# Layer 0's LSTM weights: their sums made once and kept in DRAM, and a few small operations of a step put in another order

## The chip, the cores and the metric

The kernel runs on one core of a Trainium2 chip. TensorE (PE) multiplies matrices, VectorE (DVE), ScalarE (ACT) and GpSimd (POOL) do the elementwise work, SyncE (SP) starts most transfers between DRAM and the on-chip memory SBUF. Every engine works through its own list of instructions in a fixed order; an instruction that waits holds up all that stand behind it on that engine. The metric is the device time of one execution in microseconds (us), as a median over runs. All data is float32.

## The reference, cut to what matters

Four graph layers, each `x = x + layer(relu(layernorm(x)))`. The change touches layer 0 alone: two graph convolutions, and then an LSTM over windows of p = 1, 2, 3 and 4 time steps in turn, whose last state overwrites the window's last step.

```
h = relu(einsum('ts,bsh->bth', adj, x @ Wg0 + bg0))
h = relu(einsum('ts,bsh->bth', adj, h @ Wg1 + bg1))
for p in range(1, 5):
    wins = h[:, :nw * p, :].reshape(Bv * nw, p, Hd)
    last = _lstm_last(Wih[p - 1], Whh[p - 1], bih[p - 1], bhh[p - 1], wins)
    h = h.at[:, idx, :].set(last)

# one step of the LSTM
g = x_t @ Wih.T + h @ Whh.T + bias
i, f, gg, o = split(g, 4)
c = sigmoid(f) * c + sigmoid(i) * tanh(gg)
h = sigmoid(o) * tanh(c)
```

x has 8192 rows of 256. Wih and Whh have, for each p, 1024 x 256 numbers: 1024 KB in SBUF, 8 KB in each of the 128 partitions.

## The kernel before, in words

**The order of the program.** The instructions of an engine run in the order in which they are written, but one that isn't pinned may be placed ahead of others that were written before it. `late(ins)` (line 78) pins an instruction behind the one that was written just before it for the same engine; it says nothing of those written after it, which may still move up.

**Convolutions (lines 525 to 656).** The 8192 rows go through in 16 chunks of 512 (`NCH`). A loop over rounds n = 0 to 19 starts chunk n in round n; each chunk is a generator of five pieces (norm, aggregation, first product, second product, second aggregation), so that five chunks are under way at a time. Beside each piece, from round 3 on, one piece of `tables` is written: first `edge_tables` (line 297), which prepares layer 1, then `late_tables` (line 215), which prepares layers 2 and 3. The fourth piece of `late_tables` takes a power -0.5 on POOL (line 247, tile `dinv`), and its fifth copies `dinv` on DVE (line 250, `dinv_b`). Neither is pinned. By the count of pieces, 4 in round 3 and 5 in each of rounds 4 to 13, the fourth piece of `late_tables`, which is the 55th in all, is written in the first turn of round 14.

**The weights of the LSTM (lines 494 to 516).** Each matrix product is made from seven products of quarters instead of eight. For this the four quarters a11, a12, a21, a22 of a set of weights are joined by three sums and one difference, each a 128 x 512 operation on POOL (line 512). `Weights(kind, w)` loads a set (line 500, on SP's queue) and makes them. That happens 14 times: there are two halves of the data, each with phases w = 1, 2, 3, 4, so eight sets of `ih`, and six of `hh` (w = 1 needs none). Three are loaded in the second round of the convolutions (line 652), the rest during the LSTM: `hh` when a phase ends (`phase_over`, line 945) into a single buffer, `ih` eight slots later (line 1008) into one of two.

**The LSTM (lines 660 to 1031).** PE works through slots. A slot is a gate of a step: `product` (line 745) issues its seven products in several pieces, with the accumulators `pa`, `pb`, `pc` in PSUM read between the pieces by ACT (lines 795, 800) and DVE (796, 803, 806, 813); a product that adds to `pa` again must wait until `pa` was read (line 806). `prepare` (line 700) makes a step's seven right-hand sides from its inputs: copies (line 724), differences (lines 727, 737) and one more (742). Where the step before opens a phase, POOL makes them, else ACT and DVE. At the end of a step `gate_done` makes h and its differences on DVE (lines 865 to 869).

**Memory.** The chunk buffers of the convolutions and the LSTM's tiles use the same bytes one after the other; an LSTM tile waits only for the earlier users of its own bytes. The convolutions' region holds, in this order, `xin` (4 x 4096 bytes of a partition), `g0` (10 x 4096), `wc` (5408) and `hop` (3 x 4096). The LSTM lays over it `xop` and `hop2` (2 x 9408 each), `cp` (2 x 5376) and `gp`, eight gate tiles of 5376 bytes. In the memory map the gate tiles are handed out in the order first, eighth, seventh and so on down to the second.

Of the kernel before, what the change touches and what calls it, by code (L numbers as in the profile page):

```python
# [17 lines left out]
P = 128  # L18
# [13 lines left out]
def gnn_stack_kernel(ctx: ExitStack, tc: tile.TileContext, a: dict, out: bass.AP):  # L32
# [45 lines left out]
    def late(ins):  # L78

        tc.keep_in_program_order(ins)  # L80
# [404 lines left out]
    with ExitStack() as l0:  # L485
# [5 lines left out]

        class Weights:
            def __init__(self, kind, w, keep=lambda ins: None):
                bufs = 2 if kind == "ih" else 1
                t = wsp.tile([P, 2, 4, 2, P], F32, tag=f"w{kind}", name=f"w{kind}", bufs=bufs)
                s = wsp.tile([P, 3, 4, P], F32, tag=f"s{kind}", name=f"s{kind}", bufs=bufs)
                keep(
                    nc.sync.dma_start(  # L500
                        out=t.rearrange("p k q j m -> p k (q j m)"), in_=a[f"W{kind}T"][:, w - 1]
                    )
                )
                a11, a12, a21, a22 = t[:, 0, :, 0, :], t[:, 1, :, 0, :], t[:, 0, :, 1, :], t[:, 1, :, 1, :]
                s1, s2, s4 = s[:, 0], s[:, 1], s[:, 2]
                for o, x, y, op in (
                    (s1, a21, a22, ALU.add),
                    (s2, s1, a11, ALU.subtract),
                    (s4, a12, s2, ALU.subtract),
                    (a21, a11, a21, ALU.subtract),  # L510
                ):
                    keep(nc.gpsimd.tensor_tensor(o, x, y, op))  # L512
                self.of = {1: a11, 2: a12, 3: s4, 4: a22, 5: s1, 6: s2, 7: a21}

            def __call__(self, k, q):
                return self.of[k][:, q, :]

        bias = w0.tile([P, MAX_SKIP, 8], F32, tag="bias", name="bias")
        bias2 = w0.tile([P, MAX_SKIP, 8], F32, tag="bias2", name="bias2")
# [5 lines left out]
        with ExitStack() as conv:  # L525
# [111 lines left out]

            tables = chain(edge_tables(), late_tables())
            under_way = []
            for n in range(NCH + 4):  # L640
                if n < NCH:
                    under_way.append(graph_convolutions(n))

                turns = under_way[-1:] + under_way[:-1] if n < NCH else list(under_way)
                if n == 1:
                    turns += under_way[-1:]
                for one in turns:
                    if next(one, 0) == 0:
                        under_way.remove(one)
                    if n >= 3:  # L650
                        next(tables, None)
                if n == 2:
                    weights["ih", 0], weights["ih", 1] = Weights("ih", 1), Weights("ih", 2)
                    weights["hh", 1] = Weights("hh", 2)
                    late(nc.vector.tensor_tensor(bias, bias, bias2, ALU.add))
            for _ in tables:
                pass


# [17 lines left out]
        class Step:  # L677
# [22 lines left out]
            def prepare(self, beside):  # L700
# [22 lines left out]
                def copied(to, k):  # L723
                    copy(self.as_nodes(v[:, to : to + 1]), self.nodes(slice(k, k + 1), t))  # L724

                def difference(to, k, l):
# [5 lines left out]
                    )  # L732

                copied(0, 0)
                difference(3, 2, 0)
                copied(1, 1)
                sums(
                    self.as_nodes(v[:, 5:6]), self.nodes(slice(3, 4), t), self.as_nodes(v[:, 3:4]), ALU.subtract
                )
                copied(2, 3)  # L740
                difference(4, 3, 2)
                sums(v[:, 6], v[:, 1], v[:, 5], ALU.subtract)
                self.x = {1: v[:, 0], 2: v[:, 1], 3: v[:, 2], 4: v[:, 6], 5: v[:, 3], 6: v[:, 5], 7: v[:, 4]}

# [82 lines left out]
            def gate_done(self, q):  # L827
# [28 lines left out]
                elif last:  # L856
                    if self.halved:
                        return
                    o_, g_ = (act[k][0].rearrange("p (q n) -> p q n", n=N) for k in (3, 2))
                    nc.vector.tensor_tensor(  # L860
                        self.nodes(slice(0, 4), t), self.as_nodes(o_), self.as_nodes(g_), ALU.mult
                    )
                else:
                    h = hop.tile([P, 7 * NMAX], F32, tag="h", name="lstm_h")
                    nc.vector.tensor_tensor(h[:, : 4 * N], act[3][0], act[2][0], ALU.mult)
                    v = h[:, : 7 * N].rearrange("p (q n) -> p q n", n=N)
                    nc.vector.tensor_tensor(v[:, 4:6], v[:, 2:4], v[:, 0:3:2], ALU.subtract)
                    nc.vector.tensor_tensor(v[:, 6], v[:, 3], v[:, 4], ALU.subtract)
                    nc.vector.tensor_tensor(v[:, 2], v[:, 1], v[:, 6], ALU.subtract)
                    state["h"] = {1: v[:, 0], 2: v[:, 1], 3: v[:, 3], 4: v[:, 2], 5: v[:, 4], 6: v[:, 6], 7: v[:, 5]}  # L870

# [87 lines left out]
        for slot in range(len(tasks) + 2):  # L959
# [45 lines left out]
            next(norm_steps, None)  # L1005
            while later_weights and later_weights[0][0] <= slot:
                _, ph = later_weights.pop(0)
                weights["ih", ph] = Weights("ih", phases[ph], late)
            if old:
                (at, q, k), step = old[0], steps[old[0][0]]  # L1010
                if k == len(step.gates) - 1:
                    if at + 1 == len(steps) or steps[at + 1].phase != step.phase:
                        phase_over(step.phase)
                    if step.phase == len(phases) - 1 and step.t == 1 and step.g == NGR - 1:

                        t_ = wsp.tile([P, 2, 4, 2, P], F32, tag="wih", name="x_first", bufs=2)
                        flat = t_.rearrange("p k q j m -> p k (q j m)")
                        norms1 = {}
                        for n in range(2):
                            xt = flat[:, n, :].rearrange("p (i d) -> p i d", i=4)  # L1020
# [1315 lines left out]
```

## Time and profile before

| what | us |
|---|---|
| median of 3 runs | 1943.82 (1942.74 to 1943.88) |
| the profiled execution, its own time | 1939.26 |
| span of its profile, first to last instruction | 1937.5 |
| convolutions, on PE | 0 to 190 |
| LSTM, on PE | 190 to 1253 |
| weights' sums on POOL (line 512), 56 operations | 17.9 to 33.1 and 281 to 1096 |
| one sum, 128 x 512, alone | 1.27 |
| one load of a set of weights, issue to landing | `ih` 7.0, `hh` 5.3 (medians) |

The span is what the profile shows of one execution; its own time is 1.8 us longer, which lies around it. Busy times are sums over the span; in lists of waits the three numbers are the time in all, the number of waits and the longest. In a timeline each line has start, duration, engine, line of the code and what was done, and in square brackets the idle time of the engine before it with what ended that. "SPq" and "POOLq" are the parts of SP and POOL that start transfers.

### The profile page before, as it was taken

Reading aid. Unit: us, or ns where it says so; the run is one execution under the profiler, and the core shown is the slowest. Engines: PE = TensorE matmul, PEld = TensorE weight load, DVE = VectorE, ACT = ScalarE, POOL = GpSimd, SP = SyncE. Lnnn points to the kernel's source line nnn. Section 1 sums busy time; section 2 is a strip of 40 time slices with the busy share of each in tenths; the row PEclk is TensorE's granted clock in tenths of the full one; section 3 lists DMA queues with packets and bytes.
Section 4 is the critical chain, followed back from the end, with each engine's and each line's share of the span. In section 5 each row is a group of like instructions: output and inputs, shape, how many; then the busy total and the mean of one; then the engine's idle time right before and its main releaser. Section 6 shows DMA issues by size and latency. Waiting matters only on the chain. (4 is left out here: it accounts for less than half of the span.)

```text
span 1937.5 us, 25232 instructions
## 1 busy us (share of the span) xinstructions
PE 1910.5 (99%) x9146; PEld 1394.8 (72%) x9146; DVE 1328.0 (69%) x2529; ACT 1165.4 (60%) x2199; POOL 465.5 (24%) x616
## 2 busy tenths in 40 slices
PE   9999999999999999999999999999999999999998
PEld 7777468866678884688666788876676875544787
DVE  8774675674575557756745655688788877787886
ACT  4353775664565547756645656488887556592554
POOL 3000031140040003311400200056776420000584
PEclk9999999999999999999999999999999999999999
DMA  8513000010010035000100100342323841022112
GB/s 264 186 50 109 0 23 1 1 44 0 1 44 1 1 127 178 22 1 1 44 1 1 44 1 11 99 163 104 136 61 118 329 164 57 1 72 81 43 66 88
DMA packets 63276, 132.56 MB, mean 68 GB/s; under 512 B 6576, under 2 KB 41520, under 8 KB 60848
## 3 DMA queue, kind: packets, MB, share of 16 engines
q1 hardware_dynamic: 59072, 119.22, 18.0%
q0 software_dynamic: 3472, 11.54, 1.6%
q8 instruction: 72, 1.18, 0.3%
q14 instruction: 52, 0.43, 0.1%
q10 hardware_dynamic: 608, 0.20, 0.1%
HBM read 86.10 MB, written 44.83 MB: 68 GB/s over the span
## 5 line engine op out<-in xcount | busy, mean ns | idle before, releaser
L780 ACT ACTIVATE gate<-gate,bias 128x256 f32<-128x256 f32 (+2 forms) x368 | 247.7, 678 | 174.4 <-DVE gate L796 89.5
L752 PE MATMUL pa<-xop,sih 128*128 128x256 f32 (+2 forms) x1056 | 342.3, 417 | 4.8 <-DVE gate L806 4.6
L752 PEld LDWEIGHTS pa<-xop,sih 128*128 128x128 f32 x1056 | 198.7, 190 | 74.9 <-issue 19.1
L752 PE MATMUL pc<-xop,wih 128*128 128x256 f32 (+2 forms) x736 | 251.2, 423 | 0.0
L796 DVE TENSOR_TENSOR gate<-pb,gate 128x256 f32<-128x256 f32 (+2 forms) x184 | 87.6, 476 | 226.5 <-PE pb L752 147.6
L752 PE MATMUL pa<-lstm_h,shh 128*128 128x256 f32 (+1 forms) x672 | 212.7, 398 | 0.0
L752 PEld LDWEIGHTS pc<-xop,wih 128*128 128x128 f32 x736 | 139.8, 190 | 51.2 <-issue 22.5
L813 DVE TENSOR_TENSOR gate<-pc,gate 128x256 f32<-128x256 f32 (+2 forms) x184 | 87.6, 476 | 115.1 <-PE pc L752 114.0
L752 PEld LDWEIGHTS pa<-lstm_h,shh 128*128 128x128 f32 x672 | 127.7, 190 | 30.1
L1162 ACT ACTIVATE lr<-pair 128x1024 f32<-128x1024 f32 x128 | 124.2, 1023 | 40.1 <-ACT xv L1146 16.8
L752 PE MATMUL pc<-lstm_h,whh 128*128 128x256 f32 (+1 forms) x448 | 141.8, 398 | 0.0
L795 ACT COPY gate<-pa 128x256 f32<-128x256 f32 (+2 forms) x184 | 76.0, 413 | 86.8 <-PE pa L752 86.7
L1127 PE MATMUL bank<-wlv,hT 128*128 128x260 f32 x480 | 115.6, 382 | 1.7 <-DVE xq L1138 1.7
L806 DVE TENSOR_TENSOR gate<-pa,gate 128x256 f32<-128x256 f32 (+2 forms) x184 | 87.5, 476 | 40.9 <-PE pa L752 40.1
L780 ACT ACTIVATE gate<-pa,bias 128x256 f32<-128x256 f32 (+2 forms) x184 | 93.8, 510 | 28.9 <-PE pa L752 26.9
L800 ACT COPY gate<-pa 128x256 f32<-128x256 f32 (+2 forms) x184 | 75.2, 409 | 55.7 <-PE pa L752 54.7
L752 PE MATMUL pb<-xop,wih 128*128 128x256 f32 (+1 forms) x320 | 101.8, 400 | 1.6 <-POOL xop L724 1.2
L752 PE MATMUL pa<-xop,wih 128*128 128x256 f32 (+1 forms) x320 | 101.3, 398 | 0.1
L1127 PEld LDWEIGHTS bank<-wlv,hT 128*128 128x128 f32 x480 | 88.2, 190 | 16.6 <-DVE xq L1138 3.6
L752 PEld LDWEIGHTS pc<-lstm_h,whh 128*128 128x128 f32 x448 | 85.1, 190 | 20.1
L512 POOL TENSOR_TENSOR shh<-whh 128x512 f32<-128x512 f32 x6 | 7.7, 1276 | 379.1 <-DMA whh<-in_WhhT 193.2
L724 POOL COPY xop<-hT 128x256 f32<-128x256 f32 (+1 forms) x36 | 30.8, 856 | 275.6 <-ACT gate L780 261.4
(395 smaller groups left out, 4051.1 us busy)
## 6 DMA issues: line engine op xcount, KB each, us to landing
field<-keep SPq DMA_DIRECT2D x4, 2304.0 KB, 12.3
wih<-in_WihT SPq DMA_DIRECT2D x8, 1024.0 KB, 7.0
xres<-in_x SPq DMA_DIRECT2D x16, 512.0 KB, 4.5
xa<-xres POOLq DMA_DIRECT2D x16, 512.0 KB, 4.8
xin<-xb SPq DMA_DIRECT2D x16, 512.0 KB, 3.7
h<-xb SPq DMA_DIRECT2D x16, 512.0 KB, 3.6
xin<-in_x SPq DMA_DIRECT2D x15, 512.0 KB, 5.6
out_x<-h SPq DMA_DIRECT2D x15, 512.0 KB, 2.9
```

What stands on the lines that cost most here:

```text
L512: keep(nc.gpsimd.tensor_tensor(o, x, y, op))
L724: copy(self.as_nodes(v[:, to : to + 1]), self.nodes(slice(k, k + 1), t))
L752: ins = nc.tensor.matmul(p[:, : self.N], weights[kind, self.phase](k, q), x[k], start=first_ and kind == "ih", stop=kind == "hh" or not se ...
L780: nc.scalar.activation(out, in_, AF.Tanh if q == 2 else AF.Sigmoid, bias=bias[:, self.w - 1, 2 * q + j : 2 * q + j + 1],)
L795: nc.scalar.copy(blk[0, 0], pa[:, :N])
L796: nc.vector.tensor_tensor(blk[0, 0], pb[:, :N], blk[0, 0], ALU.add)
L800: nc.scalar.copy(blk[1, 0], pa[:, :N])
L806: nc.vector.tensor_tensor(blk[1, 1], pa[:, :N], blk[1, 1], ALU.add)
L813: nc.vector.tensor_tensor(blk[1, 0], pc[:, :N], blk[1, 0], ALU.add)
L1127: ins = nc.tensor.matmul(o, hTs[n][:, k, i * P : (i + 1) * P], wlv[:, k, cols], start=k == 0, stop=k == 1)
L1162: nc.scalar.activation(lr, p, AF.Relu)
```

## The change

It has three parts. One: a set of weights and its sums now lie in one tile of 14 KB a partition. The three sets that are needed first are loaded behind round 7, each in two parts, summed once and, behind round 8, also written to DRAM (`keep_sums`). The sets of w = 3 and 4 are loaded in eight parts, from round 9 on and one part in five turns, into one buffer (`ahead`), summed on POOL and written to DRAM; loads and stores of these go through POOL's queue. In the LSTM a set comes from DRAM with its sums, in one transfer. Two: in `prepare` the second copy is made before the first difference, and the third difference before the third copy. Three: the difference of two blocks of h becomes two differences of one block, the second of them behind the next one.

```diff
@@ -491,29 +491,57 @@
 
 
+        PART = 14 * P
+        quarters0 = {
+            (kind, w): dram.tile([P, 2, PART], F32, tag=f"q{kind}{w}", name=f"q{kind}{w}")
+            for kind in ("ih", "hh")
+            for w in range(1, MAX_SKIP + 1)
+        }
+
+        def load_part(v, kind, w, part, queue):
+            at = slice(part * 4 * P, (part + 1) * 4 * P)
+            return queue.dma_start(
+                out=v[:, : 8 * P].rearrange("p (k x) -> p k x", k=2), in_=a[f"W{kind}T"][:, w - 1, :, at]
+            )
+
+        def quarters(v):
+            t = v[..., : 8 * P].rearrange("p h (k q j m) -> p h k q j m", k=2, q=2, j=2)
+            s1, s2, s4 = (
+                v[..., (8 + 2 * k) * P : (10 + 2 * k) * P].rearrange("p h (q m) -> p h q m", q=2) for k in range(3)
+            )
+            a11, a12, a21, a22 = (t[:, :, k, :, j, :] for j, k in ((0, 0), (0, 1), (1, 0), (1, 1)))
+            return a11, a12, s4, a22, s1, s2, a21
+
+        def sum_quarters(v, keep=lambda ins: None):
+            a11, a12, s4, a22, s1, s2, a21 = quarters(v)
+            for o, x, y, op in (
+                (s1, a21, a22, ALU.add),
+                (s2, s1, a11, ALU.subtract),
+                (s4, a12, s2, ALU.subtract),
+                (a21, a11, a21, ALU.subtract),
+            ):
+                keep(nc.gpsimd.tensor_tensor(o, x, y, op))
+
         class Weights:
-            def __init__(self, kind, w, keep=lambda ins: None):
-                bufs = 2 if kind == "ih" else 1
-                t = wsp.tile([P, 2, 4, 2, P], F32, tag=f"w{kind}", name=f"w{kind}", bufs=bufs)
-                s = wsp.tile([P, 3, 4, P], F32, tag=f"s{kind}", name=f"s{kind}", bufs=bufs)
-                keep(
-                    nc.sync.dma_start(
-                        out=t.rearrange("p k q j m -> p k (q j m)"), in_=a[f"W{kind}T"][:, w - 1]
-                    )
+            def __init__(self, kind, w, first_time=False, keep=lambda ins: None):
+                v = wsp.tile(
+                    [P, 2, PART], F32, tag=f"w{kind}", name=f"w{kind}", bufs=2 if kind == "ih" else 1
                 )
-                a11, a12, a21, a22 = t[:, 0, :, 0, :], t[:, 1, :, 0, :], t[:, 0, :, 1, :], t[:, 1, :, 1, :]
-                s1, s2, s4 = s[:, 0], s[:, 1], s[:, 2]
-                for o, x, y, op in (
-                    (s1, a21, a22, ALU.add),
-                    (s2, s1, a11, ALU.subtract),
-                    (s4, a12, s2, ALU.subtract),
-                    (a21, a11, a21, ALU.subtract),
-                ):
-                    keep(nc.gpsimd.tensor_tensor(o, x, y, op))
-                self.of = {1: a11, 2: a12, 3: s4, 4: a22, 5: s1, 6: s2, 7: a21}
+                self.of = quarters(v)
+                self.given = v, kind, w
+                if first_time:
+                    for part in range(2):
+                        keep(load_part(v[:, part], kind, w, part, nc.sync))
+                    sum_quarters(v, keep)
+                else:
+                    keep(nc.sync.dma_start(out=v, in_=quarters0[kind, w]))
+
+            def keep_sums(self):
+                v, kind, w = self.given
+                late(nc.gpsimd.dma_start(out=quarters0[kind, w], in_=v))
 
             def __call__(self, k, q):
-                return self.of[k][:, q, :]
+                return self.of[k - 1][:, q // 2, q % 2, :]
 
         bias = w0.tile([P, MAX_SKIP, 8], F32, tag="bias", name="bias")
         bias2 = w0.tile([P, MAX_SKIP, 8], F32, tag="bias2", name="bias2")
@@ -637,6 +665,19 @@
 
             tables = chain(edge_tables(), late_tables())
             under_way = []
+
+            def other_weights():
+                for kind, w, part in [(kind, w, part) for w in (3, 4) for kind in ("ih", "hh") for part in range(2)]:
+                    v = wc.tile([P, 1, PART], F32, tag="ahead", name="ahead")
+                    late(load_part(v[:, 0], kind, w, part, nc.gpsimd))
+                    for _ in range(3):
+                        yield
+                    sum_quarters(v, late)
+                    late(nc.gpsimd.dma_start(out=quarters0[kind, w][:, part : part + 1], in_=v))
+                    for _ in range(2):
+                        yield
+
+            ahead = other_weights()
             for n in range(NCH + 4):
                 if n < NCH:
                     under_way.append(graph_convolutions(n))
@@ -649,11 +690,17 @@
                         under_way.remove(one)
                     if n >= 3:
                         next(tables, None)
+                    if n >= 9:
+                        next(ahead, None)
+                if n == 8:
+                    for kept in weights.values():
+                        kept.keep_sums()
+                if n == 7:
+                    for kind, ph, w in (("ih", 0, 1), ("ih", 1, 2), ("hh", 1, 2)):
+                        weights[kind, ph] = Weights(kind, w, True, late)
                 if n == 2:
-                    weights["ih", 0], weights["ih", 1] = Weights("ih", 1), Weights("ih", 2)
-                    weights["hh", 1] = Weights("hh", 2)
                     late(nc.vector.tensor_tensor(bias, bias, bias2, ALU.add))
-            for _ in tables:
+            for _ in chain(tables, ahead):
                 pass
 
 
@@ -732,13 +779,13 @@
                     )
 
                 copied(0, 0)
+                copied(1, 1)
                 difference(3, 2, 0)
-                copied(1, 1)
                 sums(
                     self.as_nodes(v[:, 5:6]), self.nodes(slice(3, 4), t), self.as_nodes(v[:, 3:4]), ALU.subtract
                 )
+                difference(4, 3, 2)
                 copied(2, 3)
-                difference(4, 3, 2)
                 sums(v[:, 6], v[:, 1], v[:, 5], ALU.subtract)
                 self.x = {1: v[:, 0], 2: v[:, 1], 3: v[:, 2], 4: v[:, 6], 5: v[:, 3], 6: v[:, 5], 7: v[:, 4]}
 
@@ -864,8 +911,9 @@
                     h = hop.tile([P, 7 * NMAX], F32, tag="h", name="lstm_h")
                     nc.vector.tensor_tensor(h[:, : 4 * N], act[3][0], act[2][0], ALU.mult)
                     v = h[:, : 7 * N].rearrange("p (q n) -> p q n", n=N)
-                    nc.vector.tensor_tensor(v[:, 4:6], v[:, 2:4], v[:, 0:3:2], ALU.subtract)
+                    nc.vector.tensor_tensor(v[:, 4], v[:, 2], v[:, 0], ALU.subtract)
                     nc.vector.tensor_tensor(v[:, 6], v[:, 3], v[:, 4], ALU.subtract)
+                    nc.vector.tensor_tensor(v[:, 5], v[:, 3], v[:, 2], ALU.subtract)
                     nc.vector.tensor_tensor(v[:, 2], v[:, 1], v[:, 6], ALU.subtract)
                     state["h"] = {1: v[:, 0], 2: v[:, 1], 3: v[:, 3], 4: v[:, 2], 5: v[:, 4], 6: v[:, 6], 7: v[:, 5]}
 
@@ -1005,7 +1053,7 @@
             next(norm_steps, None)
             while later_weights and later_weights[0][0] <= slot:
                 _, ph = later_weights.pop(0)
-                weights["ih", ph] = Weights("ih", phases[ph], late)
+                weights["ih", ph] = Weights("ih", phases[ph], keep=late)
             if old:
                 (at, q, k), step = old[0], steps[old[0][0]]
                 if k == len(step.gates) - 1:
@@ -1013,8 +1061,8 @@
                         phase_over(step.phase)
                     if step.phase == len(phases) - 1 and step.t == 1 and step.g == NGR - 1:
 
-                        t_ = wsp.tile([P, 2, 4, 2, P], F32, tag="wih", name="x_first", bufs=2)
-                        flat = t_.rearrange("p k q j m -> p k (q j m)")
+                        t_ = wsp.tile([P, 2, PART], F32, tag="wih", name="x_first", bufs=2)
+                        flat = t_.rearrange("p h x -> p (h x)")[:, : 8 * D].rearrange("p (n x) -> p n x", n=2)
                         norms1 = {}
                         for n in range(2):
                             xt = flat[:, n, :].rearrange("p (i d) -> p i d", i=4)
```

## The prediction

> **What bounds the kernel.** I read the page first: busy shares and PE's clock.
>
> ```profile
> PE 1910.5 (99%) x9146; PEld 1394.8 (72%) x9146; DVE 1328.0 (69%) x2529; ACT 1165.4 (60%) x2199; POOL 465.5 (24%) x616
> ...
> PEclk9999999999999999999999999999999999999999
> ```
>
> PE works in all but 27 us (1937.5 - 1910.5), at full clock. The change leaves PE's matmuls alone, so it can save only out of these 27 us, and it costs whatever new idle time it gives to PE. POOL, which the change relieves, is busy a quarter of the time; its share as such is worth nothing. So the list of PE's waits came second. Its columns are time in all, number, longest.
>
> ```profile
> PE pa L752 <- DVE gate L806: 4.6, 8, 1.0
> ...
> PE pb L752 <- POOL xop L724: 1.2, 2, 0.6
> ```
>
> These are the LSTM's two large ones. No row has PE waiting for weights: the loads and sums were always in time. Third, the timeline around each wait. This is one at the end of phase w = 2:
>
> ```profile
> 406.24 1.27 POOL L512 TENSOR_TENSOR shh<-whh 128x512 f32<-128x512 f32 x1 [58.17 <-DMA whh<-in_WhhT]
> ...
> 406.46 1.41 DVE L742 TENSOR_TENSOR xop<-xop 128x336 f32<-128x336 f32 x1
> ...
> 408.21 0.49 DVE L806 TENSOR_TENSOR gate<-pa,gate 128x336 f32<-128x336 f32 x1
> ...
> 408.76 0.83 PE L752 MATMUL pa<-xop,sih 128*128 128x336 f32 x2 [0.80 <-DVE gate L806]
> ```
>
> Line 742 took 1.41 us where it takes 0.43 in the median; it ends at 407.87, 0.36 after the sum on POOL (406.24 + 1.27), not 0.43 after its own start. So a sum on POOL holds up a DVE operation with two inputs from SBUF, line 806 behind it is late, and PE waits. That is what the removed sums cost.
>
> **What it saves.** (a) 44 of the 56 sums (11 sets of 4) leave the LSTM. Waits of PE that stand behind such a held line 742: 0.80 at 408.76, 0.99 at 559.12, 0.93 at 941.17, together 2.7 us; at 559 the hold is 0.76 (1.19 - 0.43), so I take 2.5. The bounds are 0 (DVE finds another delay) and 2.9 (with 0.16 at 557.43).
> (b) The earlier second copy: two waits of 0.6, at 268.12 and 800.40, both for the copy that stands behind the first difference on POOL. It saves 1.2 at most. But the difference then meets the DVE operation of line 850 that starts at 266.35 (1.23 us), and the sixth product, which needs it, may wait 1.1 instead of 0.6: a loss of 1.0 for both. I take a gain of 0.5.
> (c) Line 867 in two: a block takes about 0.42 (line 868's form) against 0.67 for both, so DVE works 0.17 us longer a step, but what is needed first comes sooner and less is held at once (1.36 us at 279.04). The waits of 0.33, 0.33 and 0.32 at 281.67, 813.95 and 1101.29 may shrink: 0 to 1.0, I take 0.5.
> (d) In the convolutions, 12 sums leave the stretch 17.9 to 33.1. There DVE's line 106 took 1.22, 0.79 and 0.52 instead of 0.16. PE idles 1.9 us between 10 and 40 us (10 - 9.16 and 10 - 8.96, by windows of 10 us), partly for other reasons: 0 to 1.9, I take 0.8.
> Sum: 2.5 + 0.5 + 0.5 + 0.8 = 4.3 us.
>
> **What is hidden.** A load of 1.83 MB instead of 1.05 is 0.79 MB more, 1.9 us at the 426 GB/s of 405 to 407. The tightest use: `hh` is issued at 551.81, first used at 567.86. Together with the `ih` behind it, 3.67 MB take 8.6 us and some 2 us to start: 562.5, 5 us early. Without that cover each of the tight ones would cost what it is late. On SP's queue six loads of about 0.4 us move behind chunk 10's load; they delay chunk 11 by the 8 us of their bytes, from 72.6 to 81, and DVE reads it only at about 110.
>
> **What it adds: a chain on POOL in the convolutions.** Two lines of SP's timeline fix its start.
>
> ```profile
> 54.95 1.35 SPq L389 DMA_DIRECT2D field<-keep  x1
> 56.62 8.36 SPq L540 DMA_DIRECT2D xin<-in_x  x2
> ```
>
> The first sets are pinned behind chunk 10's load, issued at 56.62, which lands 14.6 us later, at 71.2, since the queue is full of `field` stores. Three sets, 3.15 MB, then take 8.1 us at the 387 GB/s of 64 to 66: the first is there at 73.9, the last at 79.3. POOL sums from 73.9 on: 12 x 1.27 = 15.3, to 89.2. Three stores are issued at 0.54 each (line 916), to 90.8; they move 5.5 MB, 14.2 us, to 105. The first part of the staging is loaded behind them on the same queue. Bounds: 94.7, if they don't hold it up (3.9 for 512 KB, line 540 at 71 to 115), and 107.8; I take 107.
> One part of the staging: load 3.9; four sums of 128 x 256 at 0.73 (line 737 on POOL) 2.9; store of 917 KB, which is 2.8 (`hm`, 512 KB) to 4.8 (`xa`, on POOL's queue) and 1.0 for the rest, say 4.6. There is one buffer, so nothing overlaps: 11.4 us a part, 10.6 to 12.6. The sums of parts three, four and five end at 132.7, 144.1 and 155.5, the last store lands at 194.3 (by the ends 176 to 205).
>
> **Who stands behind the waiting POOL.** (e) The root of the degrees, and DVE behind it:
>
> ```profile
> 134.25 0.58 POOL L247 TENSOR_TENSOR dinv<-dinv,half_power 128x1 f32<-128x1 f32 x1 [101.19 <-DMA a<-in_a]
> ```
> ```profile
> 135.94 0.21 DVE L250 COPY dinv_b<-dinv 128x128 f32<-128x128 f32 x1
> ...
> 136.79 0.69 DVE L618 TENSOR_TENSOR aggT<-bank,bg 128x512 f32<-128x512 f32 x1
> ```
>
> Line 247 is written in round 14, behind part five (25 turns from round 9) and ahead of part six, whose load is pinned behind it. It isn't pinned itself and may move up, but whatever part it ends up behind, POOL reaches it when that part is through. Behind part three or earlier it isn't late; behind four it is 10 us late, behind five 21. DVE then stops at line 250, and line 618, less than 1 us behind, empties a bank that PE needs. The eight PSUM banks give PE some 1 us. I take part four: a wait of 9 us, bounds 0 and 20.
> (f) Beside these, 44 sums on POOL now meet DVE between 74 and 195. In 90 to 110 DVE is busy 9.9 of 10 us, so a held operation (1.06 us for line 106 above) is passed on; elsewhere it is half idle. 0 to 5, I take 1.
> (g) The LSTM's gate tiles lie on the bytes of `ahead`. In the convolutions' region it takes 62,752 to 69,920 behind `xin`, `g0` and the rest of `wc`; the gate tiles start at 48,384, so the third and fourth and 32 bytes of the fifth lie on it. Handed out from the top, the fifth is first written by ACT at 200.06. The last store at 194.3 is in time: 0, with an end of 5 us; if (e) happens, PE comes there later as well.
>
> [...]
>
> **Sum.** -4.3 + 9 + 1 = +5.7 us. The profiled execution took 1939.26 (span 1937.5 and 1.8 around it), so 1945.0; the median of the runs stands 4.6 above it, and **1949.5** is what I predict for the median.
>
> **Rivals.**
> 1. The chain is in time for line 247 and the tiles, and the savings stay. For it: line 247 may move up to any part, and without the hold of the first load part four ends at 132. Against: the start lies behind full queues, which the order of the list need not foresee. 1943.8 - 4.3 = 1939.5; with all upper ends (2.9 + 1.2 + 1.0 + 1.9 = 7.0) 1936.8. **Faster.**
> 2. The chain is in time, but the sums in the convolutions hold DVE as they did in the LSTM. For it: they are as many and DVE is full from 90 to 110. Against: PE idles nowhere from 100 to 190. -4.3 + 3 = 1942.5: nothing to be told.
> 3. Line 247 is early in POOL's list, but the chain runs past the end of 205 and ACT waits for the tile at 200.06. It decides from the point where the last store lands after 208 (8 late, more than the savings and 3.9). At 12.6 a part and eight more operations that DVE holds for 1.06 each: 213, PE loses 12: 1943.8 - 4.3 + 12 = 1951.5. Slower.
>
> **How the numbers follow.** A measurement of this kernel can tell about 0.2%, 3.9 us, from no change. The forecast has 0.43, of which 0.04 end within 3.9 us (a short wait); rival 1 has 0.34, of which 0.03 end within; rival 2 has 0.16, rival 3 0.07. Faster 0.31, the same 0.04 + 0.03 + 0.16 = 0.23, slower 0.39 + 0.07 = 0.46. The range takes in rival 1 down to 1937 and the forecast up to line 247 behind part five (+20 + 1 - 4.3 = 1960.5): 1937 to 1961. The forecast's own range is 1942 to 1961.
>
> **What would show it.** For the forecast: an idle time of DVE of some 10 us before line 250, released by POOL's line 247, and PE idle for about as long between 134 and 160. For (a): line 742 at 0.43 at each phase's end and no wait of PE there. For (b): no wait for line 724 at 268 and 800, or a new one for line 737. For (g): ACT's wait before the gate tile of the first step. The prediction is wrong if line 247 runs within 2 us of its inputs, or if PE waits for a set of weights in the LSTM.

## The result, and the profile after

| | us |
|---|---|
| before, median of 5 runs beside those of the kernel after | 1943.82 (1942.74 to 1944.21) |
| after, median of 5 runs | 1962.97 (1960.81 to 1963.29) |
| ratio after to before, 95% interval | 1.0098 [1.0087, 1.011] |
| predicted | 1949.5, range 1937 to 1961 |
| profiled execution after, own time; span | 1962.97; 1961.2 (before 1939.26; 1937.5) |

The kernel became 19.15 us slower. The sign and the place of one loss were forecast, the size was not: +5.7 forecast, and the median lies 2 us above the range. A second loss, by the split difference of h, had been forecast as a small gain.

PE has as much work as before (9146 matmuls) and its share of the span falls; the clock shows a dent it didn't have, in the fourth slice of 49 us. The page of the kernel after:

```profile
PE 1915.6 (98%) x9146; PEld 1398.6 (71%) x9146; DVE 1329.4 (68%) x2557; ACT 1165.3 (59%) x2199; POOL 434.0 (22%) x623
...
PEclk9998999999999999999999999999999999999999
```

PE's waits after (time in all, number, longest) begin with these two. The first answers to line 806 of before, with 4.6 us in 8 waits; the second is new, and the two waits of 0.6 for POOL's copy are gone:

```profile
PE pa L799 <- DVE gate L853: 12.1, 13, 2.0
PE bank L51 <- DVE aggT L646: 10.2, 1, 10.2
```

**The wait in the convolutions.** POOL's timeline after, around the root of the degrees (start, duration, engine, line, operation, idle time before it):

```profile
137.62 0.56 POOL L676 DMA_DIRECT2D qhh<-ahead  x1 [0.30 <-POOL ahead L523]
141.78 0.73 POOL L503 DMA_DIRECT2D ahead<-in_WihT  x1 [3.60 <-DMA qhh<-ahead]
145.90 3.00 POOL L523 TENSOR_TENSOR ahead<-ahead 128x256 f32<-128x256 f32 x4 [3.40 <-DMA ahead<-in_WihT]
149.19 0.56 POOL L676 DMA_DIRECT2D qih<-ahead  x1 [0.30 <-POOL ahead L523]
149.77 0.60 POOL L247 TENSOR_TENSOR dinv<-dinv,half_power 128x1 f32<-128x1 f32 x1
```

Line 247 has its inputs at 133.38 (DVE's line 246 ends there) and runs at 149.77, behind the whole of part five. DVE's and PE's timelines show the chain behind it:

```profile
134.90 0.39 DVE L96 BATCH_NORM_STATS2 ln_st<-xin 128x6 f32<-128x256 f32 x1
150.40 0.23 DVE L250 COPY dinv_b<-dinv 128x128 f32<-128x128 f32 x1 [15.11 <-POOL dinv L247]
```
```profile
151.80 2.93 PE L51 MATMUL bank<-bdA,aggT 128*128 128x128 f32 x12 [10.24 <-DVE aggT L646]
```

DVE stands for 15.11 us, PE for 10.24: PE rode out the first 5. And PE is slow when it resumes. In windows of 1 us the figures behind the engines are the clock granted to PE (1.00 is full speed), the DMA share and GB/s:

```profile
143.00:144.00 1.00, 0.00 (x0) 0.00 (x0) 0.00 (x0) 0.00 (x0) 0.00 (x0) 0.98 0.69 94
144.00:145.00 1.00, 0.00 (x0) 0.00 (x0) 0.00 (x0) 0.00 (x0) 0.00 (x0) 0.50 0.93 369
...
156.00:157.00 1.00, 1.00 (x4) 0.81 (x3) 0.00 (x0) 1.00 (x3) 0.00 (x0) 0.50 0.75 307
157.00:158.00 1.00, 1.00 (x5) 0.78 (x4) 0.02 (x1) 0.26 (x1) 0.41 (x1) 0.69 0.07 20
158.00:159.00 1.00, 1.00 (x6) 0.90 (x5) 0.67 (x1) 0.00 (x0) 0.92 (x2) 1.00 0.90 340
```

The clock is halved 2.4 us into the wait (141.56 to 151.80) and stays so for 5.8 us of PE's work; at half clock these lose 2.9 us. Together 10.2 + 2.9 = 13.1. The LSTM's first matmul starts at 202.96 instead of 190.37, 12.6 later.

**The waits in the LSTM.** The LSTM lasts from there to layer 1's first matmul, at 1253.07 before and 1273.09 after: 1062.7 and 1070.1 us, 7.4 longer, and PE's waits for the gate's addition are 12.1 - 4.6 = 7.5 longer. (Layers 1 to 3 are 3.7 longer in this profile, 688.1 against 684.4. That goes by the chip and not by the kernel: in the runs below this stretch lasts 684.1 to 684.6 on three chips and 687.9 to 688.2 on the fourth. The profile of before is one of the short ones and stands 4.6 below the median of the runs beside the kernel after.) The longest stands at 584.60 (1.99 us). DVE's timeline in front of it:

```profile
580.53 1.04 DVE L914 TENSOR_TENSOR lstm_h<-lstm_h 128x256 f32<-128x256 f32 x1
581.49 1.07 DVE L916 TENSOR_TENSOR lstm_h<-lstm_h 128x256 f32<-128x256 f32 x1
582.49 0.85 DVE L915 TENSOR_TENSOR lstm_h<-lstm_h 128x256 f32<-128x256 f32 x1
583.26 0.41 DVE L860 TENSOR_TENSOR gate<-pc,gate 128x256 f32<-128x256 f32 x1
583.60 0.61 DVE L917 TENSOR_TENSOR lstm_h<-lstm_h 128x256 f32<-128x256 f32 x1
584.13 0.41 DVE L853 TENSOR_TENSOR gate<-pa,gate 128x256 f32<-128x256 f32 x1
```

The same place in the kernel before:

```profile
566.74 1.00 DVE L867 TENSOR_TENSOR lstm_h<-lstm_h 128x512 f32<-128x512 f32 x1
567.66 0.41 DVE L813 TENSOR_TENSOR gate<-pc,gate 128x256 f32<-128x256 f32 x1
568.00 0.53 DVE L868 TENSOR_TENSOR lstm_h<-lstm_h 128x256 f32<-128x256 f32 x1
568.46 0.41 DVE L806 TENSOR_TENSOR gate<-pa,gate 128x256 f32<-128x256 f32 x1
568.79 1.04 DVE L869 TENSOR_TENSOR lstm_h<-lstm_h 128x256 f32<-128x256 f32 x1
```

Two things differ. There are four short differences instead of three. And the gate's two additions, which stood behind the first and the second of them, stand behind the third and the fourth. Nobody wrote that down: the instructions that aren't pinned are placed when the program is built (by the planner, as it is called below), and it placed three differences in a row. A difference takes 0.41 us at its shortest (lines 914 to 917); here POOL is busy with the next step's right-hand sides from 576.79 to 583.93, and the first three take 0.85 to 1.07. So line 853 starts 3.6 us behind the first difference, where line 806 started 1.7 behind it. Which of the two is the cause, the number or the place, the trace doesn't tell.

### The profile page after: what moved, and what is told of

Read it like the earlier page. It is cut to its first block, busy times and chain, and to the rows that moved or that the text cites. A ratio compares the mean times of both kernels' runs of the same rounds, so it can differ in the third digit from the quotient of the medians.

```text
span 1961.2 us, 25289 instructions
## 1 busy us (share of the span) xinstructions
PE 1915.6 (98%) x9146; PEld 1398.6 (71%) x9146; DVE 1329.4 (68%) x2557; ACT 1165.3 (59%) x2199; POOL 434.0 (22%) x623
## 5 line engine op out<-in xcount | busy, mean ns | idle before, releaser
L799 PE MATMUL pa<-xop,wih 128*128 128x256 f32 (+2 forms) x1376 | 443.2, 412 | 12.4 <-DVE gate L853 12.1
L799 PEld LDWEIGHTS pa<-xop,wih 128*128 128x128 f32 x1376 | 258.9, 190 | 99.1 <-issue 19.6
L799 PE MATMUL pa<-lstm_h,whh 128*128 128x256 f32 (+1 forms) x896 | 283.7, 398 | 0.0
L799 PEld LDWEIGHTS pa<-lstm_h,whh 128*128 128x128 f32 x896 | 170.2, 190 | 40.2
L771 POOL COPY xop<-hT 128x256 f32<-128x256 f32 (+1 forms) x36 | 19.0, 547 | 672.8 <-DVE gate L850 282.8
L850 ACT COPY gate<-pc 128x256 f32<-128x256 f32 (+2 forms) x136 | 57.8, 425 | 53.3 <-PE pc L799 53.2
L1216 DVE SCALAR_TENSOR_TENSOR lr<-lr,fold 128x1024 f32<-128x1024 f32 x64 | 83.1, 1298 | 3.7 <-ACT lr L1210 1.7
```

The source lines that it names most:

```text
L799: ins = nc.tensor.matmul(p[:, : self.N], weights[kind, self.phase](k, q), x[k], start=first_ and kind == "ih", stop=kind == "hh" or not se ...
L850: (nc.vector.tensor_copy if not self.t and self.w > 1 else nc.scalar.copy)(blk[1, 1], pc[:, :N])
L1216: late(nc.vector.scalar_tensor_tensor(lrs[1], lrs[0], fold, lrs[1], ALU.mult, ALU.add))
```

## The experiments

The kernel before took 1939.5, 1942.8, 1939.1 and 1939.1 us on the chips of the four groups of runs, so every result stands as its ratio to the kernel before on its own chip, and as the difference to it. The expectations of the first group name times on the scale of the result, with 1943.8 for the kernel before: an expected 1950 is +6.2.

### First group: the change with one part undone

**root_off_pool.** The root leaves POOL's queue.

```diff
-            nc.gpsimd.tensor_tensor(dinv, dinv, half_power[:, 0:1], ALU.pow)
+            nc.scalar.activation(dinv, dinv, AF.Sqrt)
+            nc.vector.reciprocal(dinv, dinv)
```

> The changed kernel, with the root of the degrees (line 247) taken by ScalarE and VectorE (square root, reciprocal) instead of GpSimd; nothing else. Theory A (VectorE waited behind GpSimd's staging for the root, TensorE lost 10.2 us by it and some 3 us more at the lower clock after it): the wait before line 250 is gone, the granted clock is 1.0 throughout, the LSTM begins at 190 instead of 203, the time is 1950 (1948 to 1952). Rival 1 (the staging is late for whoever comes next: the gate tiles that lie on its buffer): ScalarE waits at the first steps of the LSTM until the last store has landed, and the time stays above 1955. Rival 2 (the operations on GpSimd slow VectorE all through the convolutions): TensorE keeps more than 5 us of idle time there, 1957 or more.

Measured 1.0035 [1.0022, 1.0048], +6.5 us: 12.7 of the 19.15 are the root's place behind the staging (the intervals of the two ratios leave some 3 us either way). PE's wait at line 646 is gone, the LSTM starts at 189.72, and no engine waits for the staging before it writes a gate tile. The 12.1 us of waits in the LSTM stay as they are.

**copies_as_before.** `prepare` makes its copies in the old order.

```diff
-                copied(1, 1)
                 difference(3, 2, 0)
+                copied(1, 1)
...
-                difference(4, 3, 2)
                 copied(2, 3)
+                difference(4, 3, 2)
```

> The changed kernel, with the copies and differences of a step's inputs in the order of the kernel before. Theory B1 (the new order puts GpSimd's differences against VectorE's large operations, line 853 is late): the waits of 0.62 at 281 and 818 vanish, those of 0.9 to 2.0 for line 853 shrink to half, the two waits for the second copy (1.2) come back: 1958 to 1960. Theory B2 (the split differences of h alone do it): the waits for line 853 stay, 1963 to 1965. Rival (larger loads of weights in the LSTM): no change, 1963.

Measured 1.0101 [1.0085, 1.0118], +19.2. The two waits of 0.6 for POOL's copy come back, and the time doesn't move: the order of the copies isn't where the LSTM loses.

**h_pair_as_before.** The undivided difference.

```diff
-                    nc.vector.tensor_tensor(v[:, 4], v[:, 2], v[:, 0], ALU.subtract)
+                    nc.vector.tensor_tensor(v[:, 4:6], v[:, 2:4], v[:, 0:3:2], ALU.subtract)
                     nc.vector.tensor_tensor(v[:, 6], v[:, 3], v[:, 4], ALU.subtract)
-                    nc.vector.tensor_tensor(v[:, 5], v[:, 3], v[:, 2], ALU.subtract)
```

> The changed kernel, with the two differences of h in one operation again, as before. Theory B2 (four short operations with two inputs each, every one of which GpSimd can hold up, stand ahead of line 853): the waits of 0.9 to 2.0 for line 853 shrink to 0.3, the time is 1957 to 1959. Theory B1 (the order of the copies alone): 1962 to 1964. Rival (larger loads): 1963.

Measured 1.0052 [1.0036, 1.0069], +10.5, which is 8.6 less than after, where 4 to 6 were expected. PE's waits for the gate's addition fall from 12.1 to 4.3 us. The split is the second loss.

**part_one_alone.** Both of these undone; left are the sums made once, and the root behind the staging.

> The changed kernel with both the order of the copies and the differences of h as before: only the sums made once and kept. Theory A with B1 or B2: the convolutions lose 12.6 us as in the changed kernel; in the LSTM TensorE idles 2.7 us less than before (the three waits behind held operations are gone, the two for the second copy are back), so 1943.8 + 12.6 - 2.7 = 1953.7 (1952 to 1955). Rival (the loads with their sums cost time in the LSTM): the LSTM stays as long as in the changed kernel, 1961 or more.

Measured 1.0042 [1.0026, 1.0059], +8.4. Less the root's 12.7 that would be a gain of 4.3; the next run measures it.

### Second group: what the first part gains, and why the split costs

**part_one_root_off_pool.** Both edits together: pair and copies as before, root off POOL.

> The kernel after with both its rearrangements of the LSTM undone (order of the copies, pair of differences) and the root of the degrees on ScalarE and VectorE; left is the first part of the change, the sums made once. If what the earlier runs took off adds up, 8.4 over the kernel before (part one alone) less 12.7 (the root's stall) is 4.3 us below the kernel before, and PE's idle time of some 10 us at line 646 is gone. If the stall and the rest are not independent (PE idles 10 us either way because something else of the staging is late), it stays between +2 and +8.

Measured 0.9982 [0.9973, 0.9992], -3.8 us. The first part does what it was predicted to do; the wait at line 646 is gone, the waits for the gate's addition are 1.9 us in 5, 2.7 less than before. Against part_one_alone (+8.4) the root's place costs 12.2 here, a second measure of the 12.7.

**split_in_kernel_before.** Nothing but line 867 in two, in the kernel before.

> The kernel before with nothing but line 867 in two. Theory: the split costs by its place in VectorE's list, three short differences ahead of the gate's additions, whatever happens in the convolutions and on GpSimd: 8 to 11 us over the kernel before, and PE's waits for the gate's addition grow from 4.6 to 11 us or more, with single ones of 2 us. Rival: it costs only together with the rest of the change (the other order of the copies, the weights' larger loads): within 2 us of the kernel before.

Measured 1.009 [1.0073, 1.0107], +18.0: the split costs without any of the rest, and nearly twice what was expected. PE's waits for line 806 are 17.5 us in 13, so 12.9 longer, with single ones of 2.9. DVE's timeline at one of these:

```profile
280.19 1.10 DVE L867 TENSOR_TENSOR lstm_h<-lstm_h 128x256 f32<-128x256 f32 x1
281.22 0.94 DVE L869 TENSOR_TENSOR lstm_h<-lstm_h 128x256 f32<-128x256 f32 x1
282.09 1.48 DVE L868 TENSOR_TENSOR lstm_h<-lstm_h 128x256 f32<-128x256 f32 x1
283.49 0.41 DVE L813 TENSOR_TENSOR gate<-pc,gate 128x256 f32<-128x256 f32 x1
283.83 1.15 DVE L870 TENSOR_TENSOR lstm_h<-lstm_h 128x256 f32<-128x256 f32 x1
284.90 0.41 DVE L806 TENSOR_TENSOR gate<-pa,gate 128x256 f32<-128x256 f32 x1
```

Here the weights' sums are still on POOL, behind `prepare`, and hold the differences too: line 868 took 1.48 us beside the sum that ran on POOL from 281.85 to 283.29, where its shortest time in the kernel before is 0.41. PE's timeline and the windows of 1 us show what a wait of that length brings:

```profile
285.37 0.79 PE L752 MATMUL pa<-xop,sih 128*128 128x256 f32 x2 [2.87 <-DVE gate L806]
```
```profile
285.00:286.00 1.00, 0.63 (x3) 0.53 (x4) 0.98 (x3) 0.00 (x0) 1.00 (x1) 0.92 0.00 0
286.00:287.00 1.00, 1.00 (x4) 0.82 (x3) 0.00 (x0) 0.80 (x2) 1.00 (x2) 0.50 0.06 16
...
289.00:290.00 1.00, 1.00 (x6) 0.88 (x5) 0.49 (x1) 0.37 (x1) 0.00 (x0) 0.87 0.00 0
```

The clock is 0.50 from about 285.8 to 289.3, and 3.4 us at half clock lose 1.7. In its LSTM the granted clock falls four times, behind the waits of 2.87, 1.89, 2.89 and 2.14: 4 x 1.7 = 6.8, and with the waits 12.9 + 6.8 = 19.7. Its LSTM is 1275.06 - 191.53 = 1083.5 long, 20.8 more than before (this profiled execution is 4.3 above the median of its kernel).

**split_behind_gates.** The kernel of root_off_pool with the four differences written later, so that the planner places them behind the gate's additions.

```diff
-                    nc.vector.tensor_tensor(v[:, 4], v[:, 2], v[:, 0], ALU.subtract)
...
+                    def differences(v=v):
+                        nc.vector.tensor_tensor(v[:, 4], v[:, 2], v[:, 0], ALU.subtract)
...
+                    apart.append([4, differences])
...
         def measure(tiles):
+            for one in list(apart):
+                one[0] -= 1
+                if not one[0]:
+                    apart.remove(one)
+                    one[1]()
```

`measure` is called twice a slot, so the four are written at its fourth call behind the step's end; DVE's list then has the additions (lines 861 and 854 of this kernel) ahead of the first difference:

```profile
563.40 0.41 DVE L861 TENSOR_TENSOR gate<-pc,gate 128x256 f32<-128x256 f32 x1
563.73 0.41 DVE L854 TENSOR_TENSOR gate<-pa,gate 128x256 f32<-128x256 f32 x1
564.06 0.41 DVE L917 TENSOR_TENSOR lstm_h<-lstm_h 128x256 f32<-128x256 f32 x1
```

> The kernel of the run root_off_pool (6.5 us over the kernel before) with the four short differences written half a slot to two slots later, so that they stand behind the gate's two additions in VectorE's list and not ahead of them; the same operations on the same data. Theory of the place: PE's waits for the gate's addition fall from 12 to below 5 us, and the time to 2 to 5 us below the kernel before. Rival, the fourth operation costs by itself (more operations held by GpSimd, more work on VectorE): the waits stay above 9 us and the time 4 to 7 us above the kernel before.

Measured 0.9971 [0.996, 0.9983], -5.3: 11.7 us less than the same operations in the other place. PE's waits for the gate's addition:

```profile
PE pa L800 <- DVE gate L854: 2.4, 5, 0.6
```

So it is the place that costs. In this place the fourth operation costs nothing that can be told: with three it is -6.1 (pair_and_copy_behind_gates below, the same kernel but for the pair).

**pair_behind_gates.** The same later place in the kernel of part_one_root_off_pool.

> The same later place for the differences in the kernel of part_one_root_off_pool (pair kept). If the place is what PE's waits for the gate's addition come from, the 4 us of them that are left fall to 1 to 2, and the time is 5 to 8 us below the kernel before. If the later place makes the next step's products wait for the differences instead, there are new waits of PE for lstm_h and the time is no better than part_one_root_off_pool.

Measured 0.997 [0.9958, 0.9981], -6.0; 1.2 us of waits in 3 are left, and none for `lstm_h`.

### Third group: how much lateness of the root is free

**root_8_late, root_24_late.** The kernel before, with 8 or 24 operations more on the root.

```diff
             nc.gpsimd.tensor_tensor(dinv, dinv, half_power[:, 0:1], ALU.pow)
+            for k in range(8):
+                nc.gpsimd.tensor_tensor(dinv, dinv, half_power[:, 0:1], (ALU.subtract, ALU.add)[k % 2])
```

> The kernel before, with eight more small operations of GpSimd on the root of the degrees behind line 247 (a half added and taken away by turns), nothing else: the root is some 4.5 us later (8 x 0.58), VectorE waits 3 to 4 us at line 250. Theory: PE is late by what VectorE is late beyond its cover, and where PE's wait passes about 2 us the granted clock falls to a half for 3.4 us and costs 1.7 more: 1 to 4 us over the kernel before, the clock 1.00 throughout if PE's wait stays below 1.8 us. Rival (PE's cover of the banks is 1 us at most, as the prediction had it): PE waits 2.5 us or more, time 3 to 6 us over.

> The same with 24 operations: the root is some 13 us later, near what it is behind part five of the staging (15.5). Theory: the whole of the stall's 12.7 us comes from the late root: PE waits 8 to 10 us at line 618, the granted clock is 0.50 from about 2 us into the wait until 4 to 6 us after its end, and the time is 10 to 13 us over the kernel before, 2 to 3 of it by the clock. Rival: the root's wait costs only itself and the rest of the 12.7 was the staging's transfers on the queues: 7 to 9 us over, at a clock of 1.00.

Measured 0.9999 [0.999, 1.0008] and 1.0002 [0.9992, 1.0011]. Both expectations missed, because the doses did: one such operation takes 0.26 us in a row and not the 0.58 of line 247, so the 24 took 6.35. DVE waits 0.97 and 3.72 us at its copy, and PE not at all. So 3.7 us of DVE's wait were free; with the 24, though, the planner had put the next emptying of a bank (line 618 of before, 620 here) ahead of the copy.

**copy_first_in_kernel_before.** Both moves of the second part alone, in the kernel before: the second copy ahead of the first difference, the third difference ahead of the third copy.

> The kernel before with nothing but the second copy ahead of the first difference on GpSimd. As the prediction had it: the two waits of 0.6 us for line 724 go, and the time is 0.5 us (-1.0 to 1.2) below the kernel before. Rival, from the runs with and without it beside the undivided pair (10.5 and 8.4 us over): it costs 1 to 3 us, by new waits of PE for the gate's addition.

Measured 1.0009 [0.9999, 1.0018], +1.0: no gain, and a loss can't be told from none. The waits for POOL's copy are gone, those for the gate's addition are 6.7 us in 11 instead of 4.6 in 8.

**pair_and_copy_behind_gates.** pair_behind_gates with the copies in the new order.

> The kernel of pair_behind_gates (6.0 us below the kernel before) with the second copy ahead of the first difference. With the differences out of the gate's way the earlier copy can only help: PE's two waits of 0.6 us for the copy go, 6.5 to 7.5 us below the kernel before. Rival: GpSimd's difference then holds VectorE at another place, as in copies beside the pair: 4 to 6 below.

Measured 0.9969 [0.9957, 0.9981], -6.1. The waits for the copy are gone and the waits for the gate's addition are 2.5 us in 5 instead of 1.2 in 3: the one for the other. Among the kernels tried this one, pair_behind_gates and split_behind_gates are the fastest, faster than before and after, and their intervals overlap.

### Fourth group: the root late for certain

**staging_a_round_later.** The kernel after, with the root behind part four of the staging, as the prediction took it.

```diff
-                    if n >= 9:
+                    if n >= 10:
                         next(ahead, None)
```

> The kernel after with the staging's turns from round 10 instead of round 9, so that line 247 stands behind part four of the staging, the case that the prediction took, and not behind part five. By the times of the kernel after (last store of part four issued at 137.6) the root comes at some 138.2, VectorE waits 3 us at line 250, and PE rides that out, as it did 3.7 us in root_24_late: no wait of PE at line 646, time 12 to 13 us below the kernel after, that is 5 to 8 over the kernel before. Rival (the prediction's: PE has 1 us of cover): PE waits 2 us or more, 8 to 11 over.

Measured 1.0031 [1.002, 1.0041], +6.6, as with the root off POOL. From its timeline:

```profile
137.66 0.23 DVE L250 COPY dinv_b<-dinv 128x128 f32<-128x128 f32 x1 [2.57 <-POOL dinv L247]
```

Line 247 runs at 137.02, DVE waits 2.57 us for it and PE not at all at line 646. Behind a part four that ends at this time the root costs nothing.

**root_60_late.** As root_8_late, with 60: the root's value comes at 150.8, without any staging.

> The kernel before with 60 small operations of GpSimd behind line 247 (0.265 us each, by root_24_late): the root at some 150.4, where it is in the kernel after, and no staging. The late root alone makes the stall: PE waits 8 to 11 us, a granted clock of 0.50 from 2 to 3 us into the wait until some 4 us or more behind its end, 11 to 14 us over the kernel before, 2 to 4 more than the wait. Rival, the staging's transfers have a part in it: 5 to 9 over.

Measured 1.0033 [1.0023, 1.0043], +7.5. From its timelines:

```profile
134.79 16.03 POOL L249 TENSOR_TENSOR dinv<-dinv,half_power 128x1 f32<-128x1 f32 x60
```
```profile
150.86 0.23 DVE L252 COPY dinv_b<-dinv 128x128 f32<-128x128 f32 x1 [10.12 <-POOL dinv L249]
```
```profile
151.19 0.66 PE L51 MATMUL bank<-ident,dinv_b 64*128 64x64 f32 x2 [4.21 <-issue]
```

This is below the 11 to 14 expected. The planner put DVE's copy behind one more operation of line 620 and two of line 597 that follow it in the kernel before, as if it reckoned with POOL's 60 operations; so DVE stood 5 us less than in the kernel after, and PE 6. PE also waits at another place, its own product with `dinv_b`. In the kernel after, where POOL's time went into transfers, it had left the copy in its old place. What the run does settle is the account: PE waits 4.21, the clock is 0.50 from 150.6 to 157.5, which loses 3.1 of PE's work, together 7.3; the LSTM starts 7.3 later than before (197.65), and the time is 7.5 longer. A late root alone, with no transfer beside it, brings both.

## Why the prediction was wrong, by its steps

**The account.** First part without the root's wait: -3.8 (part_one_root_off_pool), against a forecast of -2.3 for (a), (d) and (f). Second and third parts on top of it: 6.46 - (-3.77) = +10.2, against -1.0 for (b) and (c). The root: +12.7, against +9 for (e). These three make up the 19.15 because each is the difference between one run and the next; what stands by itself is the second measure of the root's place, 12.2, and of the split, 8.6 (h_pair_as_before). Of the 13.4 us between forecast and result, 11.2 lie with (b) and (c), most of them with (c): a cost of 8.6 where a gain of 0.5 stood. That is the step that failed.

**(a) and (d), right.** Forecast 2.5 + 0.8 = 3.3, measured 3.8 together (1.6 to 5.2 by the interval of the ratio). In that run's trace the LSTM starts 1.0 sooner than before (189.36), which is (d) less whatever (f) costs, and lasts 2.8 less (1059.9), which is (a). Line 742's successor, 789, takes 0.50 us in the mean at 128 x 336 instead of 0.70; the wait at 408 has no successor.

**(b), no gain.** Forecast a gain of 0.5, bounds a loss of 1.0 and a gain of 1.2; measured a loss of 1.0 in the kernel before (a gain of 0.2 to a loss of 3.5 by the interval), which is the lower bound, 2.1 beside the pair (10.5 against 8.4), nothing beside the split. Its two waits went, as said, and others came. They are not the lower bound's, though: that had the sixth product wait for POOL's difference, and the runs have more waits for the gate's addition (2.1 us more in copy_first_in_kernel_before).

**(c), the step that was wrong in sign.** "What is needed first comes sooner and less is held at once", a gain of 0 to 1.0, I took 0.5. Measured: a loss of 8.6 in the kernel after, 10.7 without the copies (19.2 - 8.4), 18.0 in the kernel before. The working asked what one operation holds and took DVE's list as it was. The edit changed the list: all four differences stand ahead of the gate's addition that releases the accumulator PE waits for (line 853), where two of three stood ahead of it before (line 806). The trace of before had the sizes: operations of about 1 us (line 867 took 1.00, line 869 took 1.04), and additions for which PE was already waiting 4.6 us in all. What it couldn't show is where the planner would put them, so the case with all of them ahead of the addition had to be taken as a bound. The forecast's lower bound was 0.

**(e), the mechanism right, its terms off.** The wait of line 250 for line 247, DVE's line behind it (618, now 646) and PE's wait came as forecast. Part four was the place taken, with 9 us; it was part five, the upper case, and the stall cost 12.7. That 9 comes near 12.7 is luck: behind part four, as it ran, the root costs nothing (staging_a_round_later), and the errors below work against one another.
- The start. The first sets were expected behind chunk 10's load, the first sums at 73.9. They were placed ahead of it (line 503 issued at 54.76, the sums from 62.20), so the staging was earlier: the sums of part four ended at 137.3, not 144.1, those of part five at 148.9, not 155.5.
- The part's length was well estimated: 11.4 forecast, the sums of one part to those of the next mostly 11.6 to 13.2.
- PE's cover. "The eight PSUM banks give PE some 1 us" was an estimate of mine, and wrong: 15.11 - 10.24 = 4.9 here, and 2.57 (staging_a_round_later) and 3.72 us (root_24_late) were free. PE worked on for 6.3 us after DVE had stopped (135.29 to 141.56), and its wait is put down to line 646's result, which it reads, not to a full bank. With the earlier start and this cover "behind part four" costs nothing, as the fourth group shows; "behind part five" left 10.2.
- The clock. No wait of PE in the list of before is longer than 1.3 us, so no row showed that a longer wait slows what comes after it. It was 2.9 us more.

**(f), small at most.** Forecast 1, 0 to 5. It is part of the -3.8 together with (a) and (d), and PE has no wait that points to it; not measured alone.

**(g), right.** No engine waits for the staging's last store before it writes a gate tile, with or without the root's stall; the last store was issued at 188.22 (forecast landing 194.3). Rival 3 is out. Rival 1 was to be the kernel with the root in time and gains of 4.3: that is part_one_root_off_pool, 3.8, but with the second and the third part undone.

The forecast's 0.43 hung on whether the root is late; the possibility that a small reordering is the second large loss had no case of its own. That is why the result fell outside the range although the place of the first loss was named.

## What to carry to other kernels

When an edit adds an operation to an engine whose list is planned, ask what it moves to a later place, above all operations that free an accumulator; writing the four differences later gave 11.7 us with the same work. An unpinned operation on an engine that also waits for transfers took the transfers' time as its own here (line 247 ran 16.4 us behind its inputs); keep what others need soon off that engine. Before a stall is priced, count how much work the waiting engine still has (4.9 us here), and add what the wait does to the clock afterwards (2.9 us here, behind a wait of 10.24).

## What the runs showed of the hardware

**Some waits of about 2 us were followed by half clock on PE, others weren't.** In root_off_pool a wait of 1.98 us was followed by half clock, in PE's timeline and in windows of 1 us:

```profile
571.42 0.97 PE L800 MATMUL pa<-xop,wih 128*128 128x256 f32 x2 [1.98 <-DVE gate L854]
```
```profile
571.00:572.00 1.00, 0.58 (x2) 0.54 (x3) 1.00 (x4) 0.52 (x2) 0.00 (x0) 0.85 0.00 0
572.00:573.00 1.00, 1.00 (x3) 0.78 (x3) 0.03 (x1) 0.57 (x2) 0.00 (x0) 0.50 0.06 16
...
575.00:576.00 1.00, 1.00 (x5) 0.85 (x5) 0.72 (x1) 0.37 (x1) 0.00 (x0) 0.94 0.00 0
```

From 571.7 to 575.1 that is 3.4 us at 0.50, 1.7 lost. Waits of 1.99 and 1.98 in the kernel after, of 2.02 and 1.97 in copies_as_before, and of 1.97 in root_off_pool and in staging_a_round_later left the clock at 1.00; the other one of staging_a_round_later, 1.98, and all those in split_in_kernel_before, 1.88 (in the convolutions), 1.89, 2.14, 2.87 and 2.89, were followed by a lower one. So between 1.88 and 2.02 us it went either way here, and where the clock fell, a wait of 1.98 cost 1.7 more. The time at half clock, added up over the windows, is near a multiple of 3.4 us in all these runs: 3.4 behind each of the waits of 1.88 to 2.89 that brought it, 6.8 in root_60_late, 10.2 in copies_as_before (granted clock of the whole run 0.997) and 13.7 in the kernel after (0.996); the last two stand beside waits of nearly the same length, 10.26 and 10.24 us. Why it comes in such steps, and why one wait of about 2 us brings it and the next doesn't, no run here shows.

**Small POOL operations in a row took 0.27 us each.** 60 of 128 x 1, sums and differences, took 16.03 us in root_60_late, 24 took 6.35 in root_24_late. The single power of line 247 shows 0.58 to 0.60; as it is another operation, these runs don't tell whether the row or the operation makes the difference.
